# A graph layer with gated edges on one core: the add one tile ahead and in place, the edge sums two tiles behind

## Chip, cores and metric

The kernel runs on one core of one Trainium2 chip, in fp32. The metric is the device time of one launch in microseconds. Before the change three runs took 1148.69, 1152.42 and 1154.06 us; the median is 1152.42.

## What is computed

The input is `x` with 16 batches of 1024 nodes and 256 features, and one adjacency matrix of 1024 x 1024 that is used both as `A_a` and as `A_m`. It is sparse: few entries of a column are not zero.

```
pre_u = x @ W1[:256];  pre_v = x @ W1[256:]
S[b,u,v] = sigmoid( relu(pre_u[b,u] + pre_v[b,v] + b1) . W2 + b2 )
a_t[b,v] = sum_u  S[b,u,v] * A[u,v] * x[b,u]
m_t[b,v] = (sum_u  A[u,v] * x[b,u]) * x[b,v]
z = beta1 * x + beta2 * (a_t @ Wa + ba) + beta3 * (m_t @ Wm + bm)
```

S and the two sums are needed only where A[u,v] is not zero, so the kernel works on lists of edges.

## The kernel before

**Tiles of edges.** The target nodes v are split into 8 groups of 128 and the batches into 4 groups of 4. A pair of them is a block: 32 blocks. A block is worked in two windows of 64 targets with five tiles each, and a tile has 128 edges, one on each partition. So there are 320 tiles, and the loop variable `n` counts them; `k, s = divmod(n, 10)` gives the block and the step in it.

**One tile.** `fetch(n)` is an indirect DMA from GpSimd's queue that brings 128 rows of 8 KB from `table` in DRAM: the first half of a row is pre_u of the source node for four batches, the second half is x of it. `expand(n)` (L569) multiplies on TensorE a matrix of zeros and ones (`marks`) with pre_v + b1 (`cuts`), which puts the target's row beside every edge, in the PSUM tile `pc` (two buffers). `gate(n)` adds the fetched half row and `pc` on VectorE into the tile `t` (L601, 128x1024), then for each of the four batches forms relu(t) * W2 summed over the row (L606, with an accumulator that is read out). ScalarE takes the sigmoid (L609) and scales the edge weights with it (L612, `left`); the unscaled weights come from `left_adj` (L579). `aggregate(n)` (L623) sums the fetched x rows with those weights on TensorE into the PSUM tiles `acc0` and `acc1`; in one product it makes the gated and the ungated sum. When a half window is complete, `half_end` copies its sum to SBUF (`ev`, L631).

**Around the tiles.** `turn_over` transposes `ev` on TensorE (L641), copies it into `LT` on ScalarE (L644), and VectorE multiplies the ungated half with x (L654, `times_h`). `block_end` multiplies `LT` with `w_a` and `w_m` (L672) into the PSUM tile `pz`; ScalarE copies that into `z` (L675), VectorE adds beta1 * h to it (L676), and SP stores z (L678). h of the block (`h_blk`, one buffer) is loaded at step 0 of the next block. `halves(k+1)` makes pre_v + b1 of the next block (L427) and splits it into two parts for the expansion (`X` and `low`, L461 to L468). `rows` makes pre_u of blocks that are needed later (L427, copied by L443 to `tab`) and stores it in `table`. `lists` builds the lists of edges of the eight target groups on VectorE, the last four of them in the loop in small pieces (`fill`). The last block goes through `tail`.

**Order.** The order of the instructions on each engine is written out by hand: the program is recorded under a manual schedule, and each engine follows the order in which the loop names its work. `after(step, f)` puts work on a later step, where `do(step)` calls it. Before the change, a step n runs in this order: `aggregate(n-1)`, the fetch of the tile whose place has come free, `gate(n)`, `left_adj(n+1)`, `load_mark`, `do(n)`, `expand(n+2)`, then the products and copies that belong to that step. An engine sees only its own part of this: VectorE has L601, four L606, then what `do(n)` gives it; TensorE has L623, L569, then transposes and products.

**Places and buffers.** Fetched rows have `NF` places, used in turn. A place is free when `gate` and `aggregate` of its tile are done. Small PSUM tiles of all kinds (`misc` in the profile: `p` of the products, `pt` of the transposes, `pz`, the lists' own) share two buffers.

Of the kernel before, what the change touches and what calls it, by code (L numbers as in the profile page):

```python
# [17 lines left out]
def kernel(  # L18
# [207 lines left out]

    NF = 6
    EARLY = 4  # L230
    fetched = []
    for i in range(NF):
# [146 lines left out]
    def fetch_val(n):  # L379

        for i, j in wanted[:n]:
            nc.gpsimd.indirect_dma_start(  # L382
                out=val[:, i, j:j + 1], out_offset=None, in_=adj_flat,
                in_offset=bass.IndirectOffsetOnAxis(ap=vidx[:, i, j:j + 1], axis=0),
                bounds_check=N * N - 1, oob_is_err=False)
        del wanted[:n]
# [12 lines left out]
    def after(step, f):  # L399
        due.setdefault(step, []).append(f)  # L400
# [191 lines left out]
    def fill(n, gap=True):  # L592
        for r in running:
            if r[1] == gap and r[2] <= n:
                piece_of(r, n)
                break

    def gate(n):
        k, g, vt, w, j = where(n)
        t = one.tile([P, GB, D], FP, name="t")  # L600
        nc.vector.tensor_tensor(t, fetched[n % NF][:, :GD].rearrange("p (b d) -> p b d", b=GB),  # L601
                                pcs.pop(n).rearrange("p (b d) -> p b d", b=GB), ALU.add)
        sc = wk.tile([P, GB], FP, name="sc")
        for b in range(GB):
            fill(n)
            nc.vector.scalar_tensor_tensor(t[:, b, :], t[:, b, :], 0.0, w2_b,  # L606
                                           ALU.max, ALU.mult, accum_out=sc[:, b:b + 1])
        gt = wk.tile([P, GB], FP, name="gt")
        nc.scalar.activation(gt, sc, AF.Sigmoid, bias=b2_b)  # L609
        for b in range(GB):  # L610
            m = len(QUARTERS[j])
            nc.scalar.activation(lefts[n][:, :m, b, 1, :], lefts[n][:, :m, b, 0, :], AF.Copy, scale=gt[:, b:b + 1])  # L612
# [15 lines left out]
    def half_end(n, q):  # L628

        evs[q] = one.tile([P, 2, D], FP, name=f"ev{q}")  # L630
        nc.scalar.copy(evs[q], accs.pop(q))  # L631

    def turn_over(k, w, q, step):
        if w == 0 and q == 0:
            LTs[k] = one.tile([P, DC, GB, 2, P], FP, name="LT")
        LT = LTs[k]
        pt = small("pt")
        ev = evs.pop(q)
        for i in range(4):
            r, c = divmod(i, DC)  # L640
            nc.tensor.transpose(pt[:, i * P:(i + 1) * P], ev[:, r, c * P:(c + 1) * P], ident)  # L641
        v = slice(w * W + q * U, w * W + (q + 1) * U)
        r = (w * W + q * U) // V
        nc.scalar.copy(LT.rearrange("p c b k (r v) -> p r (c b k) v", v=V)[:, r:r + 2],  # L644
                       pt.rearrange("p (r i v) -> p r i v", r=2, v=V))
        apart = k == BS - 1 and w == NW - 1
        if not apart:
            if not q:
                return
            v = slice(w * W, (w + 1) * W)  # L650

        def times_h():
            m = LT[:, :, :, 0, v]
            nc.vector.tensor_tensor(m, m, hTs[order[k]].rearrange("p b c n -> p c b n")[:, :, :, v], ALU.mult)  # L654
            if w == NW - 1 and q == 1:
                del hTs[order[k]]
        after(step + (1 if k == BS - 1 else 2), times_h)

    def block_end(k):

        g, vt = order[k]
        hb = hbs[k]
        z = big.tile([P, GB, D], FP, name="z", bufs=1)
        for h in range(2):
            for i, wt in ((1, w_a), (0, w_m)):
                step = yield
                if i:
                    pz = small("pz")
                    add_row(pz, bias_p)
                for bb in range(2):  # L670
                    for c in range(DC):
                        nc.tensor.matmul(pz[:, bb * D:(bb + 1) * D], LTs[k][:, c, 2 * h + bb, i, :], wt[:, c, :],  # L672
                                         start=False, stop=(i == 0 and c == DC - 1), skip_group_check=True)
            sl = slice(2 * h, 2 * h + 2)
            nc.scalar.copy(z[:, sl], pz.rearrange("p (b d) -> p b d", b=2))  # L675
            after(step + 2, lambda sl=sl: nc.vector.scalar_tensor_tensor(z[:, sl], hb[:, sl], be1, z[:, sl],  # L676
                                                                         ALU.mult, ALU.add))
        after(step + 3, lambda: nc.sync.dma_start(  # L678
            out[g * GB:(g + 1) * GB, vt * P:(vt + 1) * P, :].rearrange("b p d -> p b d"), z))
        del hbs[k], LTs[k]  # L680


# [43 lines left out]
    def plan(blocks, ns):  # L726

        for k, (load, *pieces) in zip(blocks, ns):
# [4 lines left out]
                     (43, 50, 52)))  # L733
    plan([(2, vt) for vt in range(NT)], ((60 + 10 * i, 68 + 10 * i, 71 + 10 * i) for i in range(NT)))
    plan([(3, vt) for vt in range(NT)], ((141, 149, 151), (149, 158, 161), *((153 + 10 * i, 161 + 10 * i, 168 + 10 * i)
                                                                             for i in range(2, NT - 1)), (223, 231, 233)))
    plan(again, ((103,), (113,), (125,), (133,)))
    begun = set(turn[:NT])
    end = parts = piece = last = None
# [2 lines left out]
        expand(n)  # L742
    left_adj(0)
    total = BS * T
    for n in range(total + 2):
        k, s = divmod(n, T)
        if 1 <= n <= total:
            aggregate(n - 1)
            fetch_val(2)
            if n - 1 + NF < total:  # L750
                fetch(n - 1 + NF)
            if n % TW in (0, MID + 1):
                half_end(n - 1, 0 if n % TW else 1)
        if n < total:
            gate(n)
            if n + 1 < total:
                left_adj(n + 1)
        if n % TW == 1 and n // TW + 1 < total // TW:
            load_mark(n // TW + 1)
        do(n)  # L760
        if n + 2 < total:
            expand(n + 2)
        if n == 1:
            w_a = load_weights(Wa, "w_a", nc.sync)
            w_m = load_weights(Wm, "w_m", nc.sync)
            bias = load_rows(bm, D, "bias", nc.sync)
            ba_b = load_rows(ba, D, "ba_b", nc.sync)
            be1 = load_rows(beta1, 1, "be1", nc.sync)
            be2 = load_rows(beta2, 1, "be2", nc.sync)
            be3 = load_rows(beta3, 1, "be3", nc.sync)  # L770
            after(10, scale_late)
        if s == 0 and 0 < k < BS:
            hbs[k - 1] = big.tile([P, GB, D], FP, name="h_blk", bufs=1)
            g, vt = order[k - 1]
            nc.sync.dma_start(hbs[k - 1], x_rows[vt * P:(vt + 1) * P, g * GB:(g + 1) * GB, :])
        if n == total - 6:
            hbs[BS - 1] = hts.tile([P, GB, DC, P], FP, name="hT").rearrange("p b c n -> p b (c n)")
            for v, m, f in tails:
                for h, o in tail_rows(x, v, m, f):
                    nc.sync.dma_start(h, o)  # L780
        for i in advance.get(n, ()):
            next(made[i], None)
        if n in start_list:
            running.append([made[start_list[n]], True, n])
            piece_of(running[-1], n)
        fill(n, False)
        if (s == 1 and 0 < k < BS) or n == total:
            turn_over(k - 1, 1, 1, n)
        if s in (3, 4, 5, 6) and 0 < k < BS:
            if s == 3:  # L790
                end = block_end(k - 1)
                next(end)
            go(end, n)
        if s == 7 and k < BS:
            turn_over(k, 0, 0, n)
            turn_over(k, 0, 1, n)
        if s == 9 and k < BS:
            turn_over(k, 1, 0, n)
        if n == total - 2:
            end = tail(tails[:2], n)  # L800
            next(end)
        elif n == total - 1:
            go(end, n)
        elif n >= total:
            end = tail([tails[2 + n - total]], n)
            next(end)
            go(end, n)
            go(end, n)
        if k + 1 < BS and s in (0, 2, 3, 5, 6):
            if s == 0:  # L810
                parts = halves(k + 1)
                next(parts)
            go(parts, n)
        if n in loads:
            if loads[n] in begun and loads[n][0] == 1:
                aside_.remove(loads[n])
            load_hT(loads[n])
            if loads[n] not in begun:
                copy_h(loads[n])
                begun.add(loads[n])  # L820
        if n in at:
            if at[n] != last:
                last = at[n]
                piece = rows(last)
                next(piece)
            go(piece, n)
        if n == 120:
            nc.gpsimd.partition_all_reduce(longest, rest, P, bass_isa.ReduceOp.max)
            after(n + 12, count_rest)
# [114 lines left out]
```

## Time and profile before

| what | value |
|---|---|
| runs | 1148.69, 1152.42, 1154.06 us, median 1152.42 |
| profiled execution | span 1165.8 us from its first to its last instruction; the page gives no other time of it |
| TensorE matmul busy | 1092.1 us |
| VectorE busy | 1056.2 us |
| ScalarE busy | 893.5 us |
| GpSimd busy | 439.9 us |
| moved by DMA | 391.40 MB, mean 336 GB/s |
| first and last add of a tile (L601) | 71.6 and 1145.4 us |

The profile is of one execution, and that one is 13 us longer than the median of the runs. Times in its rows are those of this execution. An instruction's row gives its start and its duration; instructions of one engine can overlap at their edges, so the distance between two starts says more of the pace than the duration. "Idle before" is the time in which an engine had nothing under way, and the name beside it is what ended that.

### The profile page before, as it was taken

The page shows a single profiled execution, that of the slowest core. Times are in us where ns is not written, and L with a number is a line of the kernel's source. Part 1 is how long each engine was busy: PE and PEld are TensorE (multiplying, and loading weights), DVE is VectorE, ACT ScalarE, POOL GpSimd, SP SyncE. Part 2 cuts the span into 40 slices and gives each one's busy share as a digit, 9 for nine tenths or more (in the row PEclk, how much of TensorE's full clock was granted, in tenths as well). Part 3 has the DMA queues.
Part 4 walks back from the last instruction along what each step waited for, and adds up shares of the span by engine and source line. Part 5 has one row for each costly group of instructions (what it writes and reads, how often), then busy time and mean ns, then how long its engine had stood idle before and what let it go on. Part 6 is the DMA issues. An engine that isn't in the chain of part 4 may idle for free. (4 is left out here: it accounts for less than half of the span.)

```text
span 1165.8 us, 23918 instructions
## 1 busy us (share of the span) xinstructions
PE 1092.1 (94%) x7633; PEld 723.1 (62%) x7633; DVE 1056.2 (91%) x3487; ACT 893.5 (77%) x2624; POOL 439.9 (38%) x428
## 2 busy tenths in 40 slices
PE   7867899999999999999999999999999999999986
PEld 6744666666666666666666666666666666666553
DVE  7688889888999989999999999999999999999994
ACT  2346587767887878888888888888888888888873
POOL 1556645253335333443333333333333333333330
PEclk9868899999999999999999999999999999999999
DMA  9986898999999999999999999999998998999991
GB/s 286 298 307 223 277 372 312 362 320 331 342 320 323 396 379 336 358 350 402 389 374 369 355 364 356 360 364 383 371 375 324 361 322 333 334 339 328 328 346 60
DMA packets 147048, 391.40 MB, mean 336 GB/s; under 512 B 16753, under 2 KB 105329, under 8 KB 110705
## 3 DMA queue, kind: packets, MB, share of 16 engines
q0 software_dynamic: 50016, 300.50, 68.9%
q1 hardware_dynamic: 81616, 74.99, 20.0%
q10 hardware_dynamic: 15280, 14.29, 3.7%
q8 instruction: 63, 1.03, 0.3%
q14 instruction: 73, 0.59, 0.1%
HBM read 393.78 MB, written 50.33 MB: 381 GB/s over the span
## 5 line engine op out<-in xcount | busy, mean ns | idle before, releaser
L496 POOL DMA_INDIRECT fetched<-table,uidx x320 | 341.5, 1067 | 628.3 <-PE acc L623 447.2
L606 DVE SCALAR_TENSOR_TENSOR t<-t,w_b 128x256 f32<-128x256 f32 x1280 | 478.3, 421 | 19.3 <-ACT left L612 0.5
L601 DVE TENSOR_TENSOR t<-fetched,pc 128x1024 f32<-128x1024 f32 x320 | 389.3, 1217 | 41.4 <-PE pc L569 13.9
L623 PE MATMUL acc<-fetched,left 128*32 128x256 f32 x4096 | 336.2, 391 | 31.9 <-ACT left L612 26.2
L612 ACT ACTIVATE left<-left,gt 128x32 f32<-128x32 f32 (+1 forms) x1280 | 299.3, 304 | 10.4
L569 PE MATMUL pc<-X,mark 128*128 128x512 f32 x640 | 237.6, 453 | 6.2 <-ACT mark L562 5.0
L623 PEld LDWEIGHTS acc<-fetched,left 128*32 128x32 f32 x4096 | 130.6, 109 | 179.3 <-issue 52.4
L569 PEld LDWEIGHTS pc<-X,mark 128*128 128x128 f32 x640 | 97.2, 191 | 140.0 <-issue 89.3
L609 ACT ACTIVATE gt<-sc,b_b 128x4 f32<-128x4 f32 x320 | 96.2, 301 | 43.4 <-DVE t L606 40.8
L672 PE MATMUL misc<-w_m,LT 128*128 128x256 f32 x496 | 117.2, 379 | 0.0
L672 PE MATMUL misc<-w_a,LT 128*128 128x256 f32 x496 | 117.1, 379 | 0.0
L579 ACT ACTIVATE left<-onehot,val 128x128 f32<-128x128 bf16 (+1 forms) x320 | 116.5, 364 | 0.0
L427 PE MATMUL misc<-w_v,hT 128*128 128x256 f32 x448 | 107.3, 383 | 0.0
L427 PE MATMUL misc<-w_u,hT 128*128 128x256 f32 x416 | 101.2, 390 | 5.7 <-ACT few L329 3.6
L606 DVE DVE_READ_ACCUMULATOR t<-t,w_b 128x1 f32 x1280 | 104.0, 81 | 0.0
L672 PEld LDWEIGHTS misc<-w_a,LT 128*128 128x128 f32 x496 | 93.9, 189 | 15.1
L672 PEld LDWEIGHTS misc<-w_m,LT 128*128 128x128 f32 x496 | 93.8, 189 | 14.9
L382 POOL DMA_INDIRECT val<-in_adjT_dram,vidx x80 | 85.7, 1071 | 35.1 <-issue 22.4
L427 PEld LDWEIGHTS misc<-w_v,hT 128*128 128x128 f32 x448 | 86.0, 192 | 13.9
L427 PEld LDWEIGHTS misc<-w_u,hT 128*128 128x128 f32 x416 | 79.5, 195 | 17.3 <-ACT few L329 3.7
L631 ACT COPY ev<-acc 128x512 f32<-128x512 f32 x128 | 75.5, 590 | 14.6 <-PE acc L623 4.2
L675 ACT COPY z<-misc 128x512 f32<-128x512 f32 x62 | 36.3, 586 | 58.1 <-PE misc L672 38.8
(164 smaller groups left out, 947.9 us busy)
## 6 DMA issues: line engine op xcount, KB each, us to landing
h_blk<-in_x_dram SPq DMA_DIRECT2D x31, 512.0 KB
out_dram<-z SPq DMA_DIRECT2D x31, 512.0 KB
hT<-in_xT_dram SPq DMA_DIRECT2D x28, 512.0 KB
table<-in_x_dram ACTq DMA_DIRECT2D x24, 512.0 KB
table<-tab SPq DMA_DIRECT2D x24, 512.0 KB
fetched<-table,uidx POOLq DMA_INDIRECT x320
table<-in_x_dram SPq DMA_DIRECT2D x8, 512.0 KB
table<-fetched SPq DMA_DIRECT2D x8, 512.0 KB
```

Source lines behind the costliest of these rows:

```text
L382: nc.gpsimd.indirect_dma_start(out=val[:, i, j:j + 1], out_offset=None, in_=adj_flat, in_offset=bass.IndirectOffsetOnAxis(ap=vidx[:, i, j: ...
L427: nc.tensor.matmul(p[:, bb * D:(bb + 1) * D], hT[:, 2 * h + bb, i, :], wt[:, i, :], start=(i == 0 and not begun), stop=(i == DC - 1), skip ...
L496: nc.gpsimd.indirect_dma_start(out=fetched[n % NF], out_offset=None, in_=table[g], in_offset=bass.IndirectOffsetOnAxis(ap=uidx[:, vt * NW ...
L569: nc.tensor.matmul(pcs[n][:, c], marks[n // TW][:, j * P:(j + 1) * P], cuts[k][:, w, c], start=True, stop=True)
L579: nc.scalar.activation(lefts[n][:, :m, :, 0, :], onehot[:, i, o:o + m, :].unsqueeze(2).to_broadcast([P, m, GB, V]), AF.Copy, scale=val[:, ...
L601: nc.vector.tensor_tensor(t, fetched[n % NF][:, :GD].rearrange("p (b d) -> p b d", b=GB), pcs.pop(n).rearrange("p (b d) -> p b d", b=GB), ...
L606: nc.vector.scalar_tensor_tensor(t[:, b, :], t[:, b, :], 0.0, w2_b, ALU.max, ALU.mult, accum_out=sc[:, b:b + 1])
L609: nc.scalar.activation(gt, sc, AF.Sigmoid, bias=b2_b)
L612: nc.scalar.activation(lefts[n][:, :m, b, 1, :], lefts[n][:, :m, b, 0, :], AF.Copy, scale=gt[:, b:b + 1])
L623: nc.tensor.matmul(accs[h][b * 2 * V:(b + 1) * 2 * V, r, :], left[:, i, b].rearrange("p k v -> p (k v)"), f[:, GD + b * D:GD + (b + 1) * D ...
L631: nc.scalar.copy(evs[q], accs.pop(q))
L672: nc.tensor.matmul(pz[:, bb * D:(bb + 1) * D], LTs[k][:, c, 2 * h + bb, i, :], wt[:, c, :], start=False, stop=(i == 0 and c == DC - 1), sk ...
```

## The change

The add leaves `gate` and becomes `add(n)`. It writes its sum over the first half of the fetched rows, in place of the tile `t`, and in the loop `add(n+1)` stands before `gate(n)`. `gather_in(n)` holds what used to open a step, and it is called for tile n-2 instead of n-1 until the last three steps, where it catches up. `load_mark` stands before the add. `block_end` no longer copies `pz`: VectorE adds beta1 * h to it straight from PSUM and writes the result over h, a step earlier than before, and the store takes it from there. The second window's `turn_over` moves by one step (from 9 to 0 of the next block, from 1 to 2), and its product with h follows one step after instead of two. `NF` is 7. The tiles `t` (4 KB a partition) and `z` (4 KB) are gone, and a place for fetched rows has 8 KB.

```diff
-    NF = 6
+    NF = 7
...
+    def add(n):
+        t = fetched[n % NF][:, :GD]
+        nc.vector.tensor_tensor(t, t, pcs.pop(n), ALU.add)
+
     def gate(n):
         k, g, vt, w, j = where(n)
-        t = one.tile([P, GB, D], FP, name="t")
-        nc.vector.tensor_tensor(t, fetched[n % NF][:, :GD].rearrange("p (b d) -> p b d", b=GB),
-                                pcs.pop(n).rearrange("p (b d) -> p b d", b=GB), ALU.add)
+        t = fetched[n % NF][:, :GD].rearrange("p (b d) -> p b d", b=GB)
...
-        after(step + (1 if k == BS - 1 else 2), times_h)
+        after(step + (1 if k == BS - 1 or w else 2), times_h)
...
         hb = hbs[k]
-        z = big.tile([P, GB, D], FP, name="z", bufs=1)
...
-            nc.scalar.copy(z[:, sl], pz.rearrange("p (b d) -> p b d", b=2))
-            after(step + 2, lambda sl=sl: nc.vector.scalar_tensor_tensor(z[:, sl], hb[:, sl], be1, z[:, sl],
-                                                                         ALU.mult, ALU.add))
+            after(step + 1, lambda sl=sl, pz=pz: nc.vector.scalar_tensor_tensor(
+                hb[:, sl], hb[:, sl], be1, pz.rearrange("p (b d) -> p b d", b=2), ALU.mult, ALU.add))
         after(step + 3, lambda: nc.sync.dma_start(
-            out[g * GB:(g + 1) * GB, vt * P:(vt + 1) * P, :].rearrange("b p d -> p b d"), z))
+            out[g * GB:(g + 1) * GB, vt * P:(vt + 1) * P, :].rearrange("b p d -> p b d"), hb))
...
+    add(0)
+
+    def gather_in(n):
+        aggregate(n)
+        fetch_val(2)
+        if n + NF < total:
+            fetch(n + NF)
+        if (n + 1) % TW in (0, MID + 1):
+            half_end(n, 0 if (n + 1) % TW else 1)
+
     for n in range(total + 2):
         k, s = divmod(n, T)
-        if 1 <= n <= total:
-            aggregate(n - 1)
-            fetch_val(2)
-            if n - 1 + NF < total:
-                fetch(n - 1 + NF)
-            if n % TW in (0, MID + 1):
-                half_end(n - 1, 0 if n % TW else 1)
+        if 2 <= n < total - 2:
+            gather_in(n - 2)
+        if total - 3 <= n <= total:
+            gather_in(n - 1)
+        if n % TW == 1 and n // TW + 1 < total // TW:
+            load_mark(n // TW + 1)
+        if n + 1 < total:
+            add(n + 1)
         if n < total:
             gate(n)
             if n + 1 < total:
                 left_adj(n + 1)
-        if n % TW == 1 and n // TW + 1 < total // TW:
-            load_mark(n // TW + 1)
...
-        if (s == 1 and 0 < k < BS) or n == total:
+        if (s == 2 and 0 < k < BS) or n == total:
             turn_over(k - 1, 1, 1, n)
...
-        if s == 9 and k < BS:
-            turn_over(k, 1, 0, n)
+        if (s == 0 and 0 < k < BS) or n == total - 1:
+            turn_over(k - (s == 0), 1, 0, n)
```

Besides, the load and the two u products of the last block of the fourth batch group move one step forward in the plan (222, 230, 232 instead of 223, 231, 233).

More of the change, by code (lines that the diff above doesn't have):

```diff
@@ L735 @@
     plan([(3, vt) for vt in range(NT)], ((141, 149, 151), (149, 158, 161), *((153 + 10 * i, 161 + 10 * i, 168 + 10 * i)
-                                                                             for i in range(2, NT - 1)), (223, 231, 233)))
+                                                                             for i in range(2, NT - 1)), (222, 230, 232)))
     plan(again, ((103,), (113,), (125,), (133,)))
```

## The prediction

> **What bounds the kernel now.** First the page's busy line and the table by stretches of time. I cut the span at starts of VectorE's adds (L601): from the first add to block 7, blocks 7 to 22, block 23, blocks 24 to 30, the last block. Columns: stretch, length, busy time of each engine with its instructions, granted clock, DMA share, GB/s.
>
> ```profile
> PE 1092.1 (94%) x7633; PEld 723.1 (62%) x7633; DVE 1056.2 (91%) x3487; ACT 893.5 (77%) x2624; POOL 439.9 (38%) x428
> 71.60:344.10 272.50, 249.98 (x1663) 165.47 (x1663) 239.79 (x827) 196.79 (x575) 127.23 (x123) 0.95 0.90 315
> 344.10:863.90 519.80, 512.70 (x3685) 338.53 (x3684) 492.89 (x1577) 434.37 (x1291) 195.21 (x182) 1.00 0.99 366
> 897.60:1117.50 219.90, 212.67 (x1530) 135.19 (x1531) 210.98 (x666) 185.58 (x560) 73.27 (x72) 1.00 0.92 335
> ```
>
> TensorE, VectorE and the DMA engines are all nearly full, so busy shares don't say which one sets the pace. The timelines do. VectorE late in the run (start, duration):
>
> ```profile
> 991.38 0.69 DVE L654 TENSOR_TENSOR LT<-LT,hT 128x512 f32<-128x512 f32 x1
> 991.99 1.21 DVE L601 TENSOR_TENSOR t<-fetched,pc 128x1024 f32<-128x1024 f32 x1
> 993.23 0.43 DVE L606 SCALAR_TENSOR_TENSOR t<-t,w_b 128x256 f32<-128x256 f32 x1
> ...
> 994.62 0.08 DVE L606 DVE_READ_ACCUMULATOR t<-t,w_b 128x1 f32 x1
> 994.79 1.22 DVE L601 TENSOR_TENSOR t<-fetched,pc 128x1024 f32<-128x1024 f32 x1
> 996.12 0.42 DVE L606 SCALAR_TENSOR_TENSOR t<-t,w_b 128x256 f32<-128x256 f32 x1
> ...
> 1006.52 1.22 DVE L463 TENSOR_TENSOR low<-low,X 128x1024 f32<-128x1024 f32 x1
> 1007.66 1.21 DVE L601 TENSOR_TENSOR t<-fetched,pc 128x1024 f32<-128x1024 f32 x1
> ```
>
> Look at starts. L463 and L601 have the same shape and don't depend on each other: the second starts 1.14 us after the first, before its 1.22 us are over. L601 and the first L606 do depend: the start distance is 1.24, and 1.33 where the add came straight after another tile's L606. Before such an add there is a further 0.17 from the accumulator read (994.62 to 994.79); before L654, L676 and L463 there is 0.00. So an add that follows L606 directly loses 0.17 + 0.19 = 0.36 us, another one 0.10 to 0.11. In a block of ten tiles five adds follow L606 directly (L654 twice, L676 twice and L463 once stand before the others): 5 x 0.36 + 5 x 0.105 = 2.3 us. Blocks 24 to 30 take 219.90 / 7 = 31.4 us each, several 31.29 to the hundredth, and VectorE's list without these gaps is 10 x (1.14 + 4 x 0.345) + 1.14 (low) + 2 x 0.665 (z) + 2 x 0.605 (LT) = 28.9. Nothing else stops VectorE there: **in blocks 24 to 30 VectorE's own dependence sets the pace.**
>
> TensorE in the same stretch:
>
> ```profile
> 1016.72 0.73 PE L569 MATMUL pc<-X,mark 128*128 128x512 f32 x2
> 1017.29 1.03 PE L641 MATMUL misc<-ident,ev 128*128 128x128 f32 x8
> 1018.26 1.64 PE L623 MATMUL acc<-fetched,left 128*32 128x256 f32 x16
> 1019.83 0.73 PE L569 MATMUL pc<-X,mark 128*128 128x512 f32 x2
> 1021.12 1.69 PE L623 MATMUL acc<-fetched,left 128*32 128x256 f32 x16 [0.56 <-ACT left L612]
> ```
>
> The x16 edge sums take 1.00 from start to start when nothing is late and 1.57 here: TensorE waits for the gates inside a line that counts as busy. Unhindered, by start distances: expansions 10 x 0.57, edge sums 6 x 1.00 + 4 x 0.57, transposes 1.9, the v product 2 x 2.05, block end 2 x 3.87: 27.7 us. Each half of a u product (L427 from `rows`) adds 1.82. From n = 68 to 239 there are 32 such halves, 1.86 a block: 27.7 + 3.4 = 31.1. Full blocks there measure 31.3 to 31.6. **In the middle TensorE is the bound**, and the change takes no matmul away.
>
> Waits for fetched rows are few (whole span but start and end: engine, line, waited for, us, times, longest):
>
> ```profile
> PE acc L623 <- ACT left L612: 26.2, 31, 3.5
> DVE t L601 <- DMA fetched<-table,uidx: 2.8, 3, 1.7
> ```
>
> [...] 1.22 us for L601 (reads PSUM) and for L463 (doesn't). [...]
>
> **The change part by part.**
> - **The add a tile ahead, in place.** L601 of tile n+1 stands before the four L606 of tile n, which read an add from a step ago; it writes rows that no L606 in flight touches. Both gaps should shrink to L463's 1.14: 2.3 us of VectorE time a block. In-place costs nothing extra (L463 is in place, 1.22).
> - **Edge sums two behind.** Relative to VectorE's stream this is a relabelling: tile n-2's gates still stand just before the add that frees `pc` for expansion n+2. Before and after, TensorE may start a step's sums and expansion about half a step after that add begins (gates through ScalarE: 0.3 + 4 x 0.24 us) and must be done when the add two tiles on begins: some 1.45 steps of leeway either way. So no new wait; bound: the 0.56 us above, once or twice a block, goes or stays.
> - **Seven places.** A place is held a step longer (added early) and the ring is a step longer. A fetch is issued one DVE step earlier and used one step earlier. Issue to add is 12.0 us in the median now, landing takes 8.1, the slack is 3.8 (trace's landing events in order of issue). The lead stays about 4.1 steps; at 29.4 instead of 31.4 us a block it loses 0.8 us. Cost zero while slack covers it; without that cover every late fetch stops VectorE with a gate already possible behind it.
> - **z in the rows of h.** 62 ScalarE copies of 0.59 go (36 us of an engine 77% busy; nothing on the path). L676 reads PSUM: [...] I take 0, by L601. The product's PSUM tile, one of two, is now freed by VectorE. Worst place: step 7, where the second transposes take the buffer that L676 frees after that step's gates. With TensorE the bound, count from its step 0: its steps 0 to 6 take 24.2 us, so it asks at 24.2 + 2 x 0.57 + 0.44 = 25.8; VectorE's step 7 may begin when the expansion in TensorE's step 6 is there, 21.3 + 1.14 + 0.2 = 22.6, and L676 ends 2.52 + 0.75 later, with the signal at 26.0. That is 0.2 of stall; a VectorE step, 2.9 us, is the other end, if TensorE runs ahead. I take 0.2. Behind the waiting transposes stand the next step's edge sums and expansion, and the add two steps on waits for those. The LT copy in step 2 comes one step before its product instead of two: another 0.2. On SP the load of h_blk must wait until z's store (one step earlier now) has left the same rows; behind it wait hT loads and table stores. The load is needed at L676 of step 5, 17 us later, and three such transfers took 4 us together: zero.
> - **Start and end.** The first gate waits for one more add, +1.3 us. The last three steps are as before.
>
> **Sum**, against the profiled span of 1165.8 us. Blocks 24 to 30: the limit 28.9, plus 0.4 for the PSUM waits and 0.1 for jitter beside a TensorE at 27.7: 29.4, so 7 x 2.0 = 14, and 1 in the last block. Middle, 344 to 898 us, 553.5 us for 17 blocks: TensorE's 31.1 x 17 plus 5 for list work on VectorE is 534, so 19 at most; DMA is 99% busy there and the PSUM waits take their part: a third, 6. First seven blocks: VectorE's gaps are at most 12 (list work fills many), and three engines take turns: 4. Less 1.3: 23.7. 1142.1 / 1165.8 = 0.980; times the median of the runs, 1152.4, gives **1129 us**. The profiled execution is 13 us above that median, hence the ratio.
>
> **Rivals.**
> - *The cover is thinner than thought (same).* The gaps go, but DMA at 0.92 to 0.99 holds the pace and late fetches replace them. For: the share. Against: 2.8 us of waits, and bytes fall in the late blocks. Or the 0.17 gap is the add's own wait and not the tile `t`; then only half of the 15 remains. 1147 to 1158.
> - *PSUM held by VectorE (slower).* L676 in step 7 frees the transposes' buffer late. At 1.5 us of TensorE stall a block, 31 blocks lose 46 us against at most 24 gained elsewhere: about 1172. It decides from 0.8 us a block. For: TensorE is the bound in 17 blocks. Against: there it lags, so the buffer is nearly free when it asks.
> - *All three stages gain (faster).* Early and middle recover two thirds: 15 + 13 + 8 less 1.3, ratio 0.970, 1118; everything: 1106.
>
> **How the numbers follow.** A measurement here can tell about 0.5%, 6 us, from no change. Forecast (1118 to 1144) 0.52; all three 0.15; same 0.14; slower 0.19. Faster 0.67, same 0.14, slower 0.19. The range, 1108 to 1160, leaves most of the slower case and a little below out.
>
> **What would show it.** After: L601 to L606 at about 1.14, no 0.17 before an add, blocks 24 to 30 at 29 to 30 us, middle blocks near 31.3, no copy line for z, L676 near 0.75. Wrong if L641 waits for L676 by over 0.5 us a block, if fetched rows hold up the add by over 20 us in sum, or if the late blocks stay at 31.3.

## The result and the profile after

The changed kernel takes 1167.1 us in the median of four runs (1164.4 to 1173.8), the kernel before beside it 1153.2: a ratio of 1.015, interval 1.011 to 1.019. It is slower. The profiled execution of the changed kernel, the slowest of its four, took 1173.8 us with a span of 1171.9.

The page's busy line and its row of the add (after the bar: busy time, mean ns of one, idle time before it and what ended most of that):

```profile
PE 1076.0 (92%) x7633; PEld 696.5 (59%) x7633; DVE 1025.8 (88%) x3487; ACT 858.7 (73%) x2562; POOL 445.9 (38%) x428
L600 DVE TENSOR_TENSOR fetched<-fetched,pc 128x1024 f32<-128x1024 f32 x320 | 390.1, 1219 | 105.4 <-PE pc L569 91.7
```

VectorE is busy 30 us less, ScalarE 35 us less. But the add, which waited 13.9 us for the expansion before, now waits 91.7 us. The table by stretches shows where the time is won and lost. It is cut as before at the adds that open blocks 7 and 24 (stretch, length, busy time of TensorE, its weight loads, VectorE, ScalarE and GpSimd, granted clock, DMA share, GB/s). The changed kernel:

```profile
71.70:353.50 281.80, 246.70 (x1622) 158.91 (x1621) 230.52 (x813) 186.15 (x551) 126.67 (x122) 0.91 0.88 304
353.50:913.00 559.50, 543.57 (x3950) 351.17 (x3954) 508.72 (x1675) 447.23 (x1348) 206.51 (x193) 1.00 0.98 362
913.00:1119.90 206.90, 200.03 (x1516) 123.50 (x1520) 203.38 (x668) 174.97 (x540) 77.96 (x71) 1.00 0.97 351
```

A second profile of the kernel before (experiment 1), whose execution took 1147.9 us:

```profile
71.00:328.40 257.40, 245.22 (x1664) 163.58 (x1664) 238.97 (x828) 197.16 (x575) 128.44 (x123) 0.96 0.94 333
328.40:877.00 548.60, 544.69 (x3922) 360.01 (x3920) 522.79 (x1671) 463.05 (x1373) 201.80 (x192) 1.00 0.99 367
877.00:1097.10 220.10, 212.83 (x1530) 135.28 (x1531) 211.26 (x666) 185.65 (x560) 73.96 (x72) 1.00 0.92 335
```

The late blocks went from 220.1 to 206.9 us: 13.2 us won. The first seven blocks went from 257.4 to 281.8: 24.4 lost. The middle lost another 10.9. The first profile of before, which the prediction used, had 272.5 us in the first seven blocks. That stretch differs by 15 us between two executions of one kernel, so a single pair of profiles does not fix the early loss: a second profile of the changed kernel (experiment 7), of an execution of 1157.7 us, has 274.9 there and 554.0 in the middle. Against experiment 1 that is 17.5 and 5.4 us lost.

VectorE in the late part of the changed kernel:

```profile
1001.66 0.08 DVE L608 DVE_READ_ACCUMULATOR fetched<-fetched,w_b 128x1 f32 x1
1001.67 1.22 DVE L600 TENSOR_TENSOR fetched<-fetched,pc 128x1024 f32<-128x1024 f32 x1
1002.81 0.42 DVE L608 SCALAR_TENSOR_TENSOR fetched<-fetched,w_b 128x256 f32<-128x256 f32 x1
```

From the add to the next instruction it is 1.14 us, as the prediction read from L463, and from the accumulator read to the add it is 0.01 instead of 0.17: both gaps around the add are gone. Late blocks take 29.55 us each; before, most took 31.3.

**The early loss in one chain.** The timeline of the changed kernel, in block 3:

```profile
196.63 0.95 PE L286 MATMUL misc<-R,sums 128*128 128x1 f32 x8
197.43 0.63 PE L643 MATMUL misc<-ident,ev 128*128 128x128 f32 x4
198.16 0.30 ACT L611 ACTIVATE gt<-sc,b_b 128x4 f32<-128x4 f32 x1 [1.65 <-DVE fetched L608]
198.49 0.90 ACT L614 ACTIVATE left<-left,gt 128x16 f32<-128x16 f32 x4
199.30 0.39 ACT L579 ACTIVATE left<-onehot,val 128x128 f32<-128x128 bf16 x1
199.59 0.56 ACT L646 COPY LT<-misc 128x512 f32<-128x512 f32 x1
200.20 0.79 PE L431 MATMUL misc<-b_p,unit 128*128 128x512 f32 x1 [2.14 <-ACT LT L646]
200.79 3.62 PE L427 MATMUL misc<-w_v,hT 128*128 128x256 f32 x8
205.35 0.99 PE L569 MATMUL pc<-X,mark 128*128 128x512 f32 x2
206.38 1.22 DVE L600 TENSOR_TENSOR fetched<-fetched,pc 128x1024 f32<-128x1024 f32 x1 [5.75 <-PE pc L569]
207.52 0.27 DVE L291 TENSOR_SCALAR from<-misc,base,low__108 128x1 f32<-128x1 f32 x1
```

Read it backwards from the add at 206.38, which stood still for 5.75 us. It needed the expansion at 205.35. That stood behind the v product, and the v product behind a wait of 2.14 us for a small PSUM tile. There are two such tiles. The list's product (L286) holds one until VectorE has read it, from 207.52 on. The other held the transposes of 197.43, and only the LT copy at 199.59 frees it. That copy was ready to go at 198.1, but on ScalarE it stands behind the gates of the same step and `left_adj`, and the gates waited 1.65 us for VectorE. After that wait TensorE was granted only half of its clock (0.50 from 200.2 to 204.4 us): the eight matmuls of the v product took 3.62 us. The next v product, from 209.60 us on, took 1.89 at a granted clock of 1.00. The mean granted clock of the first seven blocks is 0.91, against 0.96 in the second profile of before.

So a circle has closed: the add waits for TensorE, TensorE for a ScalarE copy, that copy for the gates, the gates for VectorE. The waits of the changed kernel's first seven blocks (what waited for what, us, times, longest):

```profile
DVE fetched L600 <- PE pc L569: 50.0, 18, 6.9
PE misc L431 <- ACT LT L646: 10.8, 3, 5.4
PE misc L427 <- ACT LT L646: 8.4, 6, 2.3
```

In neither profile of before does TensorE wait for LT in that stretch.

### The profile page after: what moved, and what is told of

It reads as the page before. It is cut to its first block, busy times and chain, and to the rows that moved or that the text cites. A ratio compares the mean times of both kernels' runs of the same rounds, so it can differ in the third digit from the quotient of the medians.

```text
span 1171.9 us, 23818 instructions
## 1 busy us (share of the span) xinstructions
PE 1076.0 (92%) x7633; PEld 696.5 (59%) x7633; DVE 1025.8 (88%) x3487; ACT 858.7 (73%) x2562; POOL 445.9 (38%) x428
## 4 chain that ended last, share of the span: by engine, by line
PE 45%; DVE 18%; ACT 17%; DMA 11%; issue 6%; POOL 1%; ACTq 1%; DVEq 0%; POOLq 0%; SPq 0%
PE misc L673 11%; PE acc L625 11%; PE misc L427 10%; DVE fetched L608 9%; PE pc L569 8%; ACT left L614 5%; DMA fetched<-table,uidx 5%; DVE fetched L600 4%; DMA h_blk<-in_x_dram 3%; PE misc L431 2%; PE misc L643 2%; ACT gt L611 2%; ACT left L579 2%; ACT ev L633 2%; ACT X L468 1%
## 5 line engine op out<-in xcount | busy, mean ns | idle before, releaser
L600 DVE TENSOR_TENSOR fetched<-fetched,pc 128x1024 f32<-128x1024 f32 x320 | 390.1, 1219 | 105.4 <-PE pc L569 91.7
L608 DVE SCALAR_TENSOR_TENSOR fetched<-fetched,w_b 128x256 f32<-128x256 f32 x1280 | 476.7, 422 | 0.0
L625 PE MATMUL acc<-fetched,left 128*32 128x256 f32 x4096 | 296.0, 391 | 5.0 <-ACT left L614 5.0
L625 PEld LDWEIGHTS acc<-fetched,left 128*32 128x32 f32 x4096 | 104.4, 109 | 143.7 <-issue 52.6
L427 PE MATMUL misc<-w_u,hT 128*128 128x256 f32 x416 | 104.8, 400 | 17.2 <-ACT LT L646 11.9
L427 PE MATMUL misc<-w_v,hT 128*128 128x256 f32 x448 | 112.5, 397 | 0.0
L608 DVE DVE_READ_ACCUMULATOR fetched<-fetched,w_b 128x1 f32 x1280 | 108.8, 85 | 0.0
L382 POOL DMA_INDIRECT val<-in_adjT_dram,vidx x80 | 89.0, 1112 | 34.0 <-issue 19.8
L427 PEld LDWEIGHTS misc<-w_u,hT 128*128 128x128 f32 x416 | 81.0, 199 | 35.0 <-ACT LT L646 17.5
L643 PE MATMUL misc<-ident,ev 128*128 128x128 f32 x512 | 80.2, 280 | 22.9 <-ACT ev L633 9.8
L427 PEld LDWEIGHTS misc<-w_v,hT 128*128 128x128 f32 x448 | 89.8, 200 | 12.9
## 6 DMA issues: line engine op xcount, KB each, us to landing
table<-fetched SPq DMA_DIRECT2D x8, 512.0 KB, 10.2
```

What stands on the lines that cost most here:

```text
L427: nc.tensor.matmul(p[:, bb * D:(bb + 1) * D], hT[:, 2 * h + bb, i, :], wt[:, i, :], start=(i == 0 and not begun), stop=(i == DC - 1), skip ...
L600: nc.vector.tensor_tensor(t, t, pcs.pop(n), ALU.add)
L625: nc.tensor.matmul(accs[h][b * 2 * V:(b + 1) * 2 * V, r, :], left[:, i, b].rearrange("p k v -> p (k v)"), f[:, GD + b * D:GD + (b + 1) * D ...
```

## Experiments

Three explanations stood against each other. **A**: the two small PSUM tiles come back through ScalarE copies behind the gates, and the change brings TensorE to them a step too early. **B**: VectorE holds the product's PSUM tile (the prediction's own slower case). **C**: the fetched rows come too late for an early add. Each kernel is compared with the kernel before on its own chip; on the chips of experiments 1 to 7 that takes 1149 us, on those of 8 to 12 it takes 1170 to 1172, so times across these groups are not compared. In the diffs, `...` marks what is left out, and words behind `#` are notes.

**1. The kernel before again.** No edit.

> The kernel before, unaltered, for a second profile: the first one's execution was 13 us longer than the median of the runs. All theories: 1149 to 1156 us; late blocks 31.3 us each. If the first seven blocks (first add to the 71st) come out shorter than the 272 us of the first profile, the loss that the change shows there is larger by that.

Measured: 1147.9 us, just under the range, and the table above. Five of the seven late blocks take 31.3 us again, the first seven blocks 257.4 instead of 272.5.

**2. Gates behind the copies.**

```diff
-            gate(n)
-            if n + 1 < total:
-                left_adj(n + 1)
+            sc = gate(n)          # VectorE's part
...
+        if n < total:             # at the end of the step
+            gate_late(n, sc)      # sigmoid and scalings
+            if n + 1 < total:
+                left_adj(n + 1)
```

> The changed kernel, with the gates on ScalarE (sigmoid and the four scalings) and left_adj named at the end of the step, behind the step's copies from PSUM, instead of in front of them. Theory A (the two small PSUM tiles are freed by ScalarE copies that stand behind the gates, and with the add a tile ahead TensorE comes to them a step too early): the waits of TensorE for the LT, X and tab copies fall from some 60 us to under 15, VectorE's wait for pc from 92 to under 40 us, time 1125 to 1150 us. Theory B (the product's PSUM tile is held by VectorE's L676): no gain, 1160 to 1172. Theory C (fetched rows come too late for the early add): no gain, 1160 to 1172, and VectorE's wait for fetched rows stays at 10 us.

Measured: ratio 1.0073 (1.0054 to 1.0091), half of the loss gone. Waits of TensorE in its first seven blocks:

```profile
PE misc L431 <- ACT LT L650: 4.7, 4, 1.6
PE acc L629 <- ACT left L618: 9.4, 11, 2.7
```

The waits for LT fell from 19.2 us to 5.4 (4.7 and a row of 0.7), and that stretch to 268.9 us. But the edge sums now wait for gates that come late, and late blocks rose to 30.2 us. Over the whole run TensorE's waits for LT fell only from 28 to 21 us and VectorE's wait for `pc` only from 91.7 to 85.4, where A expected under 15 (X and tab copies included) and under 40; the time, 1157.5 us, missed A's range too. The order of copies and gates is at work, as A says, but turning it round moves the wait instead of ending it. B and C expected no gain.

**3. z copied again, six places.** The z part is undone; its tile takes 4 of the 8 KB a partition that the seventh place has, so there are six places.

```diff
-    NF = 7
+    NF = 6
...
+            nc.scalar.copy(z[:, sl], pz.rearrange("p (b d) -> p b d", b=2))
+            after(step + 2, ...)  # z = be1 * hb + z, stored from z
```

> The changed kernel with the z part undone (ScalarE copies the product into its own tile z, VectorE adds two steps later) and, since that tile needs the room, six places. Theory A: the loss stays, 1160 to 1180. Theory B: the loss goes, under 1150. Theory C: worse than the changed kernel by 10 us or more, since a place is held a step longer out of six, with VectorE waiting for fetched rows over 30 us.

Measured: ratio 1.060 (1.055 to 1.066). Two edits in one; experiment 6 parts them. B expected under 1150. With the product copied away at once TensorE still waits 54 us for LT (29.1 and 24.9 in the two largest rows; 26.3 in the changed kernel), so these waits don't come from holding the product. What B costs by itself is read in experiment 7.

**4. The z part alone, in the kernel before.**

```diff
-            nc.scalar.copy(z[:, sl], pz...)
-            after(step + 2, ...)  # z = be1 * hb + z
+            after(step + 1, ...)  # hb = be1 * hb + pz
```

> The kernel before with the z part alone: L676 reads the product from PSUM a step earlier and writes over h, no ScalarE copy. Theory A: within 5 us of before (1148 to 1158). Theory B: slower by 8 us or more (1160 to 1172), with transposes waiting for L676 in step 7. Theory C: as before.

Measured: ratio 1.0037 (1.0015 to 1.0058), some 4 us: inside A's range and short of B's, but not nothing. TensorE's transposes wait 0.5 us for L674 in the whole run, so it isn't B. VectorE's own waits name two causes:

```profile
DVE h_blk L674 <- PE misc L671: 12.9, 9, 2.0
DVE h_blk L674 <- DMA h_blk<-in_x_dram: 2.6, 2, 2.5
```

VectorE now waits for the product, since it reads it a step earlier, and twice for h, whose load waits for the store of z from the same rows (29 times, 202 us of waiting on SP's queue).

**5. Expansion three ahead.** The add stays early, in place, with seven places and z in the rows of h. TensorE goes back to where it stood against the two other engines.

```diff
-        if 2 <= n < total - 2:
-            gather_in(n - 2)
-        if total - 3 <= n <= total:
+        if 1 <= n <= total:
             gather_in(n - 1)
-        if n % TW == 1 and n // TW + 1 < total // TW:
+        if n % TW == 0 and n // TW + 1 < total // TW:
             load_mark(n // TW + 1)
...
-        if n + 2 < total:
-            expand(n + 2)
+        if n + 3 < total:
+            expand(n + 3)         # and expand(2) after add(0), ahead of the loop
```

The second window's `turn_over` stands in steps 9 and 1 again, and `times_h` two steps after.

> The changed kernel with TensorE moved back to where it stood against VectorE and ScalarE: the add stays a tile ahead and in place, with seven places and z in the rows of h, but the edge sums come one step behind as before, the expansion is named three tiles ahead instead of two (it needs the add of the tile that VectorE has just done), load_mark comes a step earlier, and the second window's turn-over stands in steps 1 and 9 again. Theory A (the small PSUM tiles come back through copies that stand behind the gates; the change let TensorE come to them a step too early): TensorE's waits for LT, X and tab copies under 5 us, first seven blocks 250 to 260 us (before 257, changed 282), late blocks 29.4 to 29.8, time 1125 to 1140, faster than both. Theory C (rows too late for the early add) or anything else in the early add, the places or z: first seven blocks stay over 270, time 1150 to 1170.

Measured: ratio 0.989 (0.984 to 0.994), **faster than both kernels**. Its table by stretches:

```profile
69.40:329.90 260.50, 239.31 (x1639) 159.82 (x1639) 230.40 (x815) 188.38 (x553) 127.36 (x122) 0.96 0.92 330
329.90:872.50 542.60, 537.84 (x3946) 356.22 (x3944) 503.35 (x1677) 444.80 (x1345) 198.47 (x192) 1.00 1.00 374
872.50:1080.50 208.00, 205.15 (x1520) 130.32 (x1512) 202.84 (x668) 175.66 (x540) 70.49 (x70) 1.00 0.95 348
```

The time, 1139.2 us, and the late blocks, 29.7, lie in A's ranges, the first seven blocks just above. No wait of TensorE for LT is left in the first seven blocks, the clock is back at 0.96, and the late gain stays. The early add, the places and z are the changed kernel's; the loss was in where TensorE's work stands, with the turn-over and marks that go with it. Experiments 9 to 12 part the turn-over from the rest. One wait is new against the changed kernel:

```profile
DVE h_blk L676 <- PE misc L673: 45.2, 50, 3.0
```

**6. Six places in the changed kernel.** `NF = 6`, nothing else.

> The changed kernel with six places instead of seven, nothing else. If the 1219 us of the kernel with z copied come from the sixth place, this one takes 1205 to 1230 with VectorE waiting 60 us or more for fetched rows; if they come from copying z, it takes 1165 to 1180. Theory A says the first, and that late blocks go from 29.55 to about 31.

Measured: ratio 1.062 (1.057 to 1.068), like experiment 3, and

```profile
DVE fetched L600 <- DMA fetched<-table,uidx: 81.2, 86, 3.5
```

against 10.2 us with seven. The kernel with six places is starved by its transfers, so experiment 3's time was the place, not the copy. C is true of six places; at seven the rows aren't what costs.

**7. The changed kernel again.**

> The changed kernel, unaltered, once more beside the others: 1160 to 1170 us. First seven blocks 275 to 285 us, blocks 7 to 23 555 to 560, late blocks 29.55 each.

Measured: ratio 1.017 (1.012 to 1.021). Its profiled execution was its fastest, 1157.7 us: first seven blocks 274.9 and middle 554.0, both just under what was expected, late 206.7. Its TensorE waits 19.3 us for LT in the first seven blocks, as the first profile's does. Two of its rows price case B. TensorE in step 7 of two blocks:

```profile
795.95 1.28 PE L643 MATMUL misc<-ident,ev 128*128 128x128 f32 x8
...
827.91 1.28 PE L643 MATMUL misc<-ident,ev 128*128 128x128 f32 x8
829.12 1.07 PE L625 MATMUL acc<-fetched,left 128*32 128x256 f32 x16
```

The transposes take 1.21 us from start to start; before it was 0.97, and it is 0.96 again in most middle blocks of experiment 3, which copies the product. So this is the wait for L676, 0.24 us in most blocks; where it is long enough for the profile to name what ended it, it names L676 (5 waits, 5.0 us over the run).

**8. L676 a step later, in the kernel of experiment 5.** `after(step + 2, ...)` instead of `after(step + 1, ...)`.

> The kernel with the expansion three ahead, with L676 two steps after its product instead of one (the product's PSUM tile is then held a step longer). There VectorE waits 45 us for the product, in 50 waits. If those waits are on the path (VectorE sets the pace in the late blocks): late blocks fall from 29.71 to about 29.0 to 29.4 and the time by 3 to 8 us, to 1128 to 1136. If the longer hold of one of the two small tiles costs TensorE as much, or the waits had been covered, the time stays within 3 us of 1139; if it costs more, middle blocks rise above 31.6 and the time goes to 1145 or more.

Measured: ratio to before 1.0067 (1.0042 to 1.0091), where experiment 9 on the same chip has 0.9966. Late blocks take 30.7 us and full middle blocks 32.55. That is the third of the expected cases. The waits for the product go, and in their place:

```profile
PE misc L643 <- ACT LT L646: 27.3, 25, 2.2
```

One of two small tiles held a step longer leaves one for everything else. It is the same shortage as in the changed kernel, made by another route.

**9 and 11. The turn-over as in the change, in the kernel of experiment 5.** Steps 0 and 2 instead of 9 and 1, `times_h` one step after.

> The kernel with the expansion three ahead, but with the second window's turn-over where the change has it (steps 0 of the next block and 2, product with h one step later). Theory A (TensorE's place against ScalarE and VectorE is what costs): within 6 us of the 1139 of the kernel it is made from, TensorE's waits for LT copies under 8 us. If instead the moved turn-over is what costs in the changed kernel (transposes and the v product now in one step, LT one step before its use): first seven blocks over 270, time 1150 to 1165.

> The same with the second window's turn-over where the change has it, on the same chip. If the moved turn-over costs by itself (VectorE waited 25 us for the LT copy in the first run of it): ratio 0.004 to 0.010 above the unmoved one's, late blocks 30.4 against 29.7. If the difference of the first runs was the chip: within 0.002, and late blocks alike.

**10 and 12. Experiment 5's kernel and the changed kernel on the same chip as 11.**

> The kernel with the expansion three ahead, unaltered, beside the next two on one chip: the comparisons so far came from chips on which the kernel before took 1149 and 1170 us. Theory A: ratio to before 0.985 to 0.993 again; first seven blocks at least 10 us shorter than those of the changed kernel on the same chip, late blocks 29.7.

> The changed kernel on the same chip: ratio to before 1.011 to 1.020, late blocks 29.5, first seven blocks 270 to 285 us, TensorE waiting 20 us or more for LT copies there.

Experiment 9 gave 0.9966 (0.9944 to 0.9987) on a chip where 5 had not run, so its time stays open by itself; TensorE waits 6.4 us for LT in it, within A's 8. The last three ran on one chip:

| kernel | ratio to before | median, us | profiled run, us | first seven | middle | late |
|---|---|---|---|---|---|---|
| 10: three ahead | 0.982 (0.977 to 0.986) | 1150.6 | 1159.9 | 273.5 | 556.4 | 208.0 |
| 11: with the turn-over moved | 1.000 (0.997 to 1.003) | 1170.5 | 1170.5 | 274.7 | 558.8 | 212.9 |
| 12: changed kernel | 1.011 (1.007 to 1.016) | 1182.3 | 1188.9 | 288.8 | 567.7 | 206.8 |

Some of this lies outside what was expected: the ratio of experiment 10 is below 0.985, and 12 takes more than 285 us in its first seven blocks.

The moved turn-over costs by itself: 0.018 between 10 and 11, beyond the 0.010 expected at most. Between 5 and 9, on two chips, it is 0.007, so its size is uncertain. The trace shows how it costs: VectorE's product with h waits for the LT copy, in experiment 11

```profile
DVE LT L656 <- ACT LT L646: 23.1, 17, 5.6
```

against 6.3 us in experiment 10.

The other part, 0.011 between 11 and 12, comes with TensorE's shift: sums two behind, expansion only two ahead of an early add. The waits for LT in the first seven blocks follow the shift and not the turn-over: 0.7 us in 10, 4.1 in 11, 18.6 in 12 (20 or more was expected). How many us of that stretch they are worth is less certain: it is 14 us longer in 12 than in 11, but the profiled execution of 12 is 6.6 us longer than its median. With TensorE shifted, the turn-over could not stay where it was without standing right behind the sums it transposes; that pairing was not run. Nor was a kernel with a third small tile, which would test A directly.

## Why the prediction was wrong

- **Gaps around the add: right.** 1.14 us was forecast from L463 and measured. Late blocks: 29.4 forecast, 29.55 measured. Their gain, 14 forecast, is 13.0 against the first profile and 13.2 against the second.
- **"So no new wait": the step that failed.** The leeway of TensorE was worked out over two loops, `pc` with the add and gates with edge sums, and both stay as they were. The third loop, small PSUM tile, ScalarE copy, gates, VectorE, is not in it; of the small tiles the prediction followed only the product's. There the change takes a step away: TensorE may begin its step n while VectorE is in step n-1, but the copy that frees a small tile in step n still stands behind the gates of step n, which need VectorE's step n. Costed at zero; measured at 19 us of TensorE idle in the first seven blocks, with a lower clock (0.91 and 0.94 in the two profiles, 0.95 and 0.96 before). The stretch takes 17.5 to 24.4 us longer than in experiment 1.
- **First seven blocks: minus 4 forecast,** plus 9.3 on the first profile's 272.5, plus 24.4 on the second's 257.4 (2.4 and 17.5 with experiment 7's profile). What made that stretch long in the first profile is not known; TensorE does not wait for LT there. In the chain above a list product holds one of the two small tiles for some 11 us. That the list products are what makes the shortage bite there is likely but not shown: no run goes without them.
- **Middle: minus 6 forecast, plus 6.0 and plus 10.9 measured, plus 5.4 in experiment 7 against experiment 1.** TensorE is the bound there, as said, but the 31.3 to 31.6 us that the prediction took for full blocks are VectorE's, read from its adds. TensorE falls behind VectorE meanwhile: from the add of tile 7 to the transposes of step 7 it is 3.9 us in block 17 of experiment 1 and 6.0 in block 22. Its own full block, here between the transposes of step 7, takes 31.96:

```profile
775.79 1.04 PE L641 MATMUL misc<-ident,ev 128*128 128x128 f32 x8
...
807.75 1.03 PE L641 MATMUL misc<-ident,ev 128*128 128x128 f32 x8
```

  In the changed kernel it takes 31.96 again (795.95 to 827.91, experiment 7). The one late gate of a block is gone (0.58 us in the edge sums: what "goes or stays" went), and as much has come back: 0.29 in the transposes, 0.18 around the matmul that opens a v product, 0.10 in the expansions. Experiment 5 has neither and takes 31.39; the prediction's 27.7 and two halves of a u product make 31.3, so the size was right. What the middle lost lies in blocks 7 to 13 and in block 23: blocks 14 to 22 take 286.2 us together in experiment 1, 286.7 and 285.2 in the two profiles of the changed kernel. TensorE waits 7.0 and 5.3 us for LT in the middle of these two profiles; before, it has no such wait.
- **PSUM held by VectorE, the slower rival: right sign and near in time (1172; its own 46 us lost and 24 gained give 1174), by luck, since it names the wrong tile.** Its own wait is 0.24 us in most blocks, far below the 0.8 from which it would decide; in experiment 3 the waits for LT stay without it.
- **z in the rows of h, costed at zero: 4 us** in experiment 4. The load of h comes late there (2.6 us in 2 waits), and VectorE meets the product before it is done (12.9 us in 9). The PSUM read itself shows no cost, as forecast: L676 takes 746 ns in the median from SBUF (the kernel before) and 747 from PSUM (the changed kernel).
- **Seven places, costed at zero: right** as far as can be told (VectorE waits 10.2 us for rows, 2.8 before), and six would have cost 55 us.
- The forecast of 1129 took 15 us from the late blocks and the last one, 6 from the middle and 4 from the first seven. The kernel of experiment 5, with TensorE put back, gains 1.1% and 1.8% on two chips. Its profile has the late blocks 12.1 and the middle 6.0 us shorter than experiment 1's, and the first seven 3.1 longer: the early term is not seen in it. The 1106 for "everything" leaves out the 1.3 us of the start.

## What to carry to other kernels

When one engine's work is moved a step ahead, list every loop that it closes through the others, the return of shared buffers included, and count the steps in each; the loop that lost one showed up here as 19 us in which TensorE waited for ScalarE's LT copies in the first seven blocks. Count a buffer as free when the instruction that frees it has run, not when that instruction could run: the LT copy of the chain had its transposes at 198.1 us and started at 199.59, behind the gates in its engine's order. If a reordering gains in one stretch and loses in another, keep the order that gained and put the other engines back where they stood against it. A block's length read from one engine is the pace of the others only while its lead over them doesn't change; in the middle of experiment 1 VectorE's lead grew from 3.9 to 6.0 us.

## What was not expected of the hardware

- After waits of nearly the same length TensorE was granted different clocks. After the wait of 2.14 us in the chain above the granted clock was 0.50 and the eight matmuls of a v product took 3.62 us, 1.73 more than the 1.89 of the next one. In the same profile the eight matmuls of a u product came at 292.53 us after a wait of 2.06 us, at a granted clock of 1.00, and took 1.99. What decides between the two is not shown.
- The same kernel took 1149 us on two chips and 1170 to 1172 on two others. The late blocks of experiments 5 and 10 take 29.7 us on both kinds. The first seven blocks and the middle differ in their profiles (260.5 and 542.6 us against 273.5 and 556.4), but the profiled execution of 5 was 7.6 us below its median and that of 10 was 9.4 above, so part of this is the spread between executions. The cause is not shown.
